# An attention kernel with Strassen's products: another order of the seven products, and q/k factors run in VectorE's pause before the softmax

## The chip, the cores and the metric

The kernel runs on one core of one Trainium2 chip. The metric is the device time of one execution in microseconds (us); of several executions the median is given. Smaller is better. All data is float32.

## The reference, cut to what matters

```python
# x: (4, 1024, 1024), cond: (4, 1024), 16 heads of 64
scale, shift = split(cond[:, None] @ W_emb + b_emb)
xn  = rms_norm(x, g_norm) * (1 + scale) + shift
q, k, v = heads(xn @ W_qkv)                  # 1024 -> 3 x 1024
q, k = rms_norm(q, g_q), rms_norm(k, g_k)    # over the 64 of a head
o = softmax(q @ k.T * 64**-0.5) @ v
x = x + o + o @ W_out
return x + causal_conv(x, w=cond, b)         # four taps along the tokens
```

The change touches the product `xn @ W_qkv` and the norm of q and k. The weights g_q and g_k are folded into k; what is left of the norm is one factor per token and head, 1 / sqrt(mean of squares), here called the factor of q and k.

## The kernel before, in words

**Work and stages.** For each of four batches the normalized, modulated x is written transposed to DRAM as four blocks (A11, A12, A21, A22) and sums of them (S1 to S4), in the form of Strassen and Winograd. A *double* is four heads: two *pairs* of heads of 128 columns each. Its q, k and v (2 x 384 columns, 1024 tokens) come from seven block products P1 to P7, each of four pieces of 128 tokens: 28 pieces a double (`PRODUCTS`, L480 to L485), 16 doubles. A piece is a group of matmuls into one of three PSUM accumulators (`ps_m`) and an eviction by ScalarE or VectorE (`Double.piece`, L537). The combined weight blocks T1 to T4 of a double's columns are made once, in batch 0 (`Weights.combine`, L468: four subtractions and four stores), and read back from DRAM (`load_w`, L499).

**The pair.** A pair's q and k come in two halves g of 512 tokens. `ENDS` (L570) says which product completes which half. `done` (L394) then books four steps: squares on ScalarE, sums on VectorE, a root on ScalarE, and `scale` on VectorE (L417: a reciprocal and one multiplication of the half by its factors). `transposes` (L422) turn q and k by TensorE, some pieces after the last product of the half (`LEADS`, L837); it calls `need`, which runs what is still booked for this half at once.

**The unit.** A unit (`Unit`, L573) is 512 queries of a pair; a double has four. It makes eight score tiles [128 keys, 2 heads, 512 queries]: TensorE, copy by ScalarE (L592), running maximum by VectorE (L601). Then POOL makes one all-reduce of the maximum over the partitions (L606), ScalarE copies it to PSUM into one of the two buffers of the score tiles (L615), and for each tile VectorE subtracts it (L620, the shift), ScalarE takes the exponential (L624) and POOL adds it to the sum (L626). In the next unit the values products (L646) and the product of ones with the sum (`tot`, L666) follow.

**The order.** Instructions of TensorE, VectorE, ScalarE and POOL run in the order in which the program issues them. The program keeps a clock of its own (`clock`, L92): each step that feeds TensorE moves it by an estimate (2.65 for a piece, 0.9 for a score tile), `defer` books a step for a due time, `tick` runs what is due. `defer_quiet` (L115) moves a due time out of the stretch in which shifts and exponentials run. `softmax` (L628) books the all-reduce at 2.6 after the last scores and the first shift at 7.6. While a unit of double n runs, seven pieces of double n+1 are placed between its steps (`between`, L940): unit i of the double gets pieces 7i to 7i+6, nearly all of them after the last scores. From batch 1 on a unit also carries one block of the output product and the convolution of the batch before; in the last batch these blocks are spread unevenly.

In the order of before, of the two pairs of a double the second (`px`) gets its first half from P2 (piece 7) and its second from P4 (piece 27); the first (`py`) gets its halves from P3 (piece 19) and P7 (piece 23).

```python
PRODUCTS: P1 P1 P2 P2 P1 P1 P2 P2, then 4 x P6, P5, P3, P7, P4
WEIGHTS = {"P1": -8, "P2": -4, "P6": 0, "P5": 6, "P3": 8, "P7": 12, "P4": 16}
ENDS = {"P2": (1, 0), "P3": (0, 0), "P7": (0, 1), "P4": (1, 1)}
LEADS = ((4, 4), (7, 7))          # [pair][half], in pieces
QUIET_QK = ((0, 0), (1, 1))
```

Of the kernel before, what the change touches and what calls it, by code (L numbers as in the profile page):

```python
# [10 lines left out]
F32 = mybir.dt.float32  # L11
AF = mybir.ActivationFunctionType
ALU = mybir.AluOpType
# [8 lines left out]
def kernel(  # L22
# [87 lines left out]
        clock[0] += us  # L110
        flush(lambda e: e[0] <= clock[0])

    loud = [0.0, 0.0]

    def defer_quiet(delay, key, step):  # L115

# [66 lines left out]
    class Norm:  # L183


        def __init__(self, b, tiles):
            self.b, self.tiles = b, tiles
            n = len(tiles)
            self.name = f"{b}_{tiles[0]}"
            self.ss = small.tile([P, NT * 2], F32, tag="ss", name=f"ss_{self.name}")  # L190
            self.ss = self.ss[:, : n * 2].rearrange("p (i g) -> p i g", i=n)
            self.rn = small.tile([P, NT], F32, tag="rn", name=f"rn_{self.name}")[:, :n]

# [109 lines left out]

    mod_sb = []
    x0 = {}
    homes = [("qTy0", 1), ("kTy0", 1), ("qTy1", 1), ("kTy1", 1), ("vy0", 1), ("vy1", 1), ("vx1", 2), ("vx1", 2)]

    def first_tokens(h):

# [62 lines left out]
    class Pair:  # L372
# [2 lines left out]
            self.qk = {}  # L375

        def begin(self):
            self.qT, self.kT, self.v = {}, {}, {}

        def open(self, g):  # L380

            b, c = self.b, self.c
            if g not in self.qk:
                self.qk[g] = apool.tile([P, HT, 2 * P], F32, tag="qk", name=f"qk_{b}_{c}_{g}", bufs=3)
                tag = f"v{'yx'[c % 2]}{g}"
                self.v[g] = apool.tile([P, HT, P], F32, tag=tag, name=f"v_{b}_{c}_{g}", bufs=1 + c % 2)

        def parts(self, t):

# [4 lines left out]
        def done(self, g):  # L394
            steps = ((0.6, self.squares), (2.2, self.sums), (4.2, self.root), (6.2, self.scale))
            for delay, step in steps:
                later = defer_quiet if step == self.scale and QUIET_QK[self.c % 2][g] else defer
                later(delay, ("qk", self.b, self.c, g), lambda step=step: step(g))


        def squares(self, g):
# [5 lines left out]
                self.sq.append(sq)  # L407

        def sums(self, g):
            self.ms = small.tile([P, 4 * HT], F32, tag="ms", name=f"ms_{self.b}_{self.c}_{g}")  # L410
            for i in range(2):
                nc.vector.tensor_reduce(self.ms[:, 2 * HT * i : 2 * HT * (i + 1)], self.sq[i], AX.X, ALU.add)

        def root(self, g):
            nc.scalar.activation(self.ms, self.ms, AF.Sqrt, bias=eps, scale=1.0 / D)

        def scale(self, g):  # L417
            qk = self.qk[g].rearrange("p t (h d) -> p (t h) d", d=D)
            nc.vector.reciprocal(self.ms, self.ms)
            nc.vector.tensor_mul(qk, qk, self.ms.unsqueeze(2).to_broadcast([P, 4 * HT, D]))  # L420

        def transposes(self, g, s):  # L422

            b, c = self.b, self.c
            need("qk", b, c, g)
            tp = ps_m.tile([P, HN], F32, tag="m", name=f"qkt_{b}_{c}_{g}_{s}")
            for i in range(HT):
                nc.tensor.transpose(  # L428
                    tp[:, i * P : (i + 1) * P], self.qk[g][:, i, s * P : (s + 1) * P], ident
                )  # L430
            tag = ("qT", "kT")[s]
            bufs = 2 if c % 2 and g == 0 else 1
            dst = apool.tile([P, HN], F32, tag=f"{tag}{'yx'[c % 2]}{g}", name=f"{tag}_{b}_{c}_{g}", bufs=bufs)
            if s:
                nc.scalar.activation(dst, tp, AF.Identity, scale=gqk)
            else:
                nc.scalar.copy(dst, tp)
            (self.qT, self.kT)[s][g] = dst
# [10 lines left out]
    class Weights:  # L449
# [6 lines left out]
        def load(self):  # L456
            d, k = self.d, self.k
            self.b = {}
            for kh in range(2):
                for y in range(2):  # L460
                    t = apool.tile([P, HN], F32, tag="ob", name=f"b_{self.name}_{kh}_{y}", bufs=8)
                    self.b[kh, y] = t[:, :W3]
                    for s, src in enumerate(w_block(kh, 2 * d + 1 - y, k)):
                        nc.sync.dma_start(t[:, s * P : (s + 1) * P], src)
            if d:
                defer_quiet(5.0, ("B", d), self.combine)

        def combine(self):  # L468
            b11, b12, b21, b22 = (self.b[kh, y] for kh in range(2) for y in range(2))
# [10 lines left out]
    PRODUCTS = []  # L480
    for ts in ((0, 1), (2, 3)):
        PRODUCTS += [("P1", A11, t) for t in ts] + [("P2", A12, t) for t in ts]
    for name, a in (("P6", S2), ("P5", S1), ("P3", S4), ("P7", S3), ("P4", A22)):
        PRODUCTS += [(name, a, t) for t in range(HT)]
    NPR = len(PRODUCTS)  # L485

    WEIGHTS = {"P1": -8, "P2": -4, "P6": 0, "P5": 6, "P3": 8, "P7": 12, "P4": 16}
    TIME = 2.65

    class Double:  # L490
        def __init__(self, n):
# [5 lines left out]
            self.w, self.a, self.u2, self.u4 = {}, {}, {}, {}  # L497

        def load_w(self, name):  # L499
            b, d = self.b, self.d  # L500
            w = wpool.tile([P, KH, W3], F32, tag="w", name=f"w_{b}_{d}_{name}", bufs=3)
            self.w[name] = w
            block = {"P1": (0, 2 * d + 1), "P2": (1, 2 * d + 1), "P3": (1, 2 * d)}.get(name)
# [33 lines left out]
        def piece(self, i):  # L537

            name, place, t = PRODUCTS[i]
            py, px = self.pairs  # L540
            pm = ps_m.tile([P, 512], F32, tag="m", name=f"pqkv_{self.n}_{name}_{t}")[:, :W3]
            w, a = self.w[name], self.a[place, t // 2]
            for k in range(KH):
                nc.tensor.matmul(  # L544
                    pm,
                    a[:, k, t % 2 * P : (t % 2 + 1) * P],
                    w[:, k, :],
                    start=(k == 0),
                    stop=(k == KH - 1),
                )  # L550
            tick(TIME)
            if name == "P1":
                self.u2[t] = apool.tile([P, W3], F32, tag="u2", name=f"u2_{self.n}_{t}", bufs=HT)
                nc.scalar.copy(self.u2[t], pm)
            elif name == "P6":
                nc.vector.tensor_add(self.u2[t], self.u2[t], pm)
            elif name == "P5":
                self.u4[t] = apool.tile([P, W3], F32, tag="u4", name=f"u4_{self.n}_{t}", bufs=HT)
                nc.vector.tensor_add(self.u4[t], self.u2[t], pm)
            else:  # L560
                pr, g, u = {"P2": (px, 0, self.u2), "P3": (py, 0, self.u4), "P7": (py, 1, self.u4), "P4": (px, 1, self.u2)}[name]
                for dst, at in pr.parts(g * HT + t):
# [377 lines left out]
    def between(p):  # L940
# [6 lines left out]
        pl = last_plan if b == B - 1 else plan  # L947
        ks = range(sum(pl[:i]), sum(pl[: i + 1])) if b else ()
        slots[0].append((0.45, store))
# [149 lines left out]
```

## Time and profile before

| | us |
|---|---|
| three executions: median (lowest, highest) | 2998.19 (2994.96, 3001.06) |
| the profiled execution: its time | 2998.24 |
| its span, first to last instruction | 2996.4 |
| TensorE busy in it (PE) | 2844.6 |
| VectorE busy (DVE) | 2227.7 |
| ScalarE busy (ACT) | 1701.0 |
| GpSimd busy (POOL) | 1407.5 |

The mean clock that TensorE was granted was 0.982 of its full one. How to read the lines that follow: a group is line, engine, operation, output<-inputs, shape and count, then busy us and mean ns of one, then the idle time of the engine just before them and what ended it. In a timeline a line begins with its start and its length in us. `A <- B: total, times, longest` in a list of waits means that engine and line A stood idle until B was done. "issue" is time in which an engine waited for nothing that the profile shows.

The units of batch 0 begin at 167.5 us; those of batch 1 at 803.2, of batch 3 at 2203.1; the last double begins at 2691.8.

### The profile page before, as it was taken

Reading aid. Unit: us, or ns where it says so; the run is one execution under the profiler, and the core shown is the slowest. Engines: PE = TensorE matmul, PEld = TensorE weight load, DVE = VectorE, ACT = ScalarE, POOL = GpSimd, SP = SyncE. Lnnn points to the kernel's source line nnn. Section 1 sums busy time; section 2 is a strip of 40 time slices with the busy share of each in tenths; the row PEclk is TensorE's granted clock in tenths of the full one; section 3 lists DMA queues with packets and bytes.
Section 4 is the critical chain, followed back from the end, with each engine's and each line's share of the span. In section 5 each row is a group of like instructions: output and inputs, shape, how many; then the busy total and the mean of one; then the engine's idle time right before and its main releaser. Section 6 shows DMA issues by size and latency. Waiting matters only on the chain.

```text
span 2996.4 us, 32118 instructions
## 1 busy us (share of the span) xinstructions
PE 2844.6 (95%) x10601; PEld 1343.9 (45%) x10601; DVE 2227.7 (74%) x2563; ACT 1701.0 (57%) x2237; POOL 1407.5 (47%) x574
## 2 busy tenths in 40 slices
PE   7789898999999999999999999999999999999899
PEld 3444444444444444444444444544444444443344
DVE  3468787877867777887777777887877768787863
ACT  3145666665655657665565656765565656565432
POOL 2035553455554454455455544535555455554420
PEclk9999999999999999999999999999999999999999
DMA  7855454543333344643433444643443333323333
GB/s 274 283 167 161 145 179 142 180 138 99 115 116 117 123 145 159 193 151 124 125 115 116 131 138 136 200 147 103 130 146 105 99 92 127 109 78 110 106 95 113
DMA packets 401661, 414.51 MB, mean 138 GB/s; under 512 B 40480, under 2 KB 331608, under 8 KB 401496
## 3 DMA queue, kind: packets, MB, share of 16 engines
q1 hardware_dynamic: 401496, 412.46, 43.6%
q8 instruction: 85, 1.39, 0.2%
q14 instruction: 80, 0.66, 0.1%
HBM read 336.88 MB, written 75.48 MB: 138 GB/s over the span
## 4 chain that ended last, share of the span: by engine, by line
PE 69%; DVE 15%; ACT 5%; DMA 4%; POOL 3%; issue 3%; SPq 1%; DVEq 0%; POOLq 0%; ACTq 0%
PE pqkv_P L544 29%; PE po L776 12%; PE s L584 12%; PE pav L646 11%; DVE sp L620 3%; DVE mx L601 3%; DVE y L808 3%; POOL sum L626 2%; ACT sp L592 2%; PE qkt L428 1%; DVE r L299 1%; DMA a<-scrA 1%; DVE b L476 1%; PE tot L666 1%; POOL mb L606 1%
## 5 line engine op out<-in xcount | busy, mean ns | idle before, releaser
L544 PE MATMUL pqkv_P<-w_P,a 128*128 128x384 f32 x3584 | 1225.2, 495 | 30.9 <-ACT r L230 9.0
L626 POOL TENSOR_TENSOR sum<-sum,sp 128x1024 f32<-128x1024 f32 x384 | 993.3, 2587 | 41.7 <-ACT sp L624 14.9
L544 PEld LDWEIGHTS pqkv_P<-w_P,a 128*128 128x128 f32 x3584 | 674.5, 193 | 517.9 <-issue 71.8
L592 ACT COPY sp<-s 128x1024 f32<-128x1024 f32 x512 | 511.4, 1015 | 468.1 <-PE s L584 376.6
L620 DVE TENSOR_TENSOR sp<-sp,mbp 128x1024 f32<-128x1024 f32 x512 | 604.1, 1212 | 70.8 <-ACT mbp L615 70.5
L601 DVE TENSOR_TENSOR mx<-mx,sp 128x1024 f32<-128x1024 f32 x384 | 519.6, 1353 | 172.1 <-ACT sp L592 146.5
L606 POOL PARTITION_ALL_REDUCE mb<-mx x64 | 207.7, 3245 | 834.8 <-DVE mx L601 690.1
L624 ACT ACTIVATE sp<-sp 128x1024 f32<-128x1024 f32 x512 | 525.4, 1054 | 124.0 <-DVE sp L620 119.3
L584 PE MATMUL s<-qT,kT 64*128 64x512 f32 x2048 | 523.7, 628 | 44.1 <-ACT sp L592 28.1
L646 PE MATMUL pav<-sp,v 128*64 128x512 f32 x2048 | 472.1, 603 | 0.0
L776 PE MATMUL po<-ob,wo 128*128 128x512 f32 x992 | 438.8, 595 | 2.4 <-DMA ob<-scrO 1.6
L626 POOL TENSOR_TENSOR sum<-sp,sp 128x1024 f32<-128x1024 f32 x64 | 151.3, 2364 | 535.2 <-ACT sp L624 364.0
L808 DVE SCALAR_TENSOR_TENSOR y<-x,cols,y 128x512 f32<-128x512 f32 x192 | 334.8, 1744 | 76.8 <-ACT y L796 72.3
L584 PEld LDWEIGHTS s<-qT,kT 64*128 64x128 f32 x2048 | 174.0, 188 | 316.3 <-issue 186.1
L646 PEld LDWEIGHTS pav<-sp,v 128*64 128x64 f32 x2048 | 136.8, 138 | 322.2 <-issue 301.6
L776 PEld LDWEIGHTS po<-ob,wo 128*128 128x128 f32 x992 | 184.1, 191 | 211.2 <-issue 205.0
L601 DVE TENSOR_TENSOR mx<-sp,sp 128x1024 f32<-128x1024 f32 x64 | 120.7, 1886 | 81.0 <-ACT sp L592 81.0
L563 DVE TENSOR_TENSOR qk<-u,pqkv_P 128x256 f32<-128x256 f32 x256 | 105.7, 413 | 94.2 <-PE pqkv_P L544 87.9
L794 ACT COPY x<-po 128x512 f32<-128x512 f32 x64 | 37.5, 585 | 238.1 <-PE po L776 221.7
L615 ACT COPY mbp<-mb 128x1024 f32<-128x1024 f32 x64 | 65.2, 1019 | 81.3 <-POOL mb L606 80.9
L420 DVE TENSOR_TENSOR qk<-qk,ms 128x1024 f32<-128x1024 f32 x64 | 106.5, 1664 | 2.2
L428 PE MATMUL qkt<-ident,qk 128*128 128x128 f32 x512 | 81.8, 283 | 27.2 <-DVE qk L420 27.1
(82 smaller groups left out, 1636.6 us busy)
## 6 DMA issues: line engine op xcount, KB each, us to landing
a<-scrA SPq DMA_DIRECT2D x220, 512.0 KB
w_P<-scrB SPq DMA_DIRECT2D x64, 768.0 KB
w_P<-in_L_cond_W_qkv_dram SPq DMA_DIRECT2D x144, 256.0 KB
wo<-in_L_cond_W_out_dram SPq DMA_DIRECT2D x128, 256.0 KB
scrA<-r SPq DMA_DIRECT2D x29, 896.0 KB
xc<-in_x_dram SPq DMA_DIRECT2D x64, 256.0 KB
out_dram<-ot SPq DMA_DIRECT2D x64, 256.0 KB
rec<-scrR SPq DMA_DIRECT2D x124, 128.0 KB
```

The source lines that it names most:

```text
L428: nc.tensor.transpose(tp[:, i * P : (i + 1) * P], self.qk[g][:, i, s * P : (s + 1) * P], ident)
L544: nc.tensor.matmul(pm, a[:, k, t % 2 * P : (t % 2 + 1) * P], w[:, k, :], start=(k == 0), stop=(k == KH - 1),)
L584: nc.tensor.matmul(ps[:, h, :], pr.kT[kt // HT][h * D : (h + 1) * D, kt % HT * P : (kt % HT + 1) * P], pr.qT[self.half][h * D : (h + 1) * ...
L592: nc.scalar.copy(sp, ps)
L601: nc.vector.tensor_max(self.mx, self.mx if kt > 1 else self.sp[0], self.sp[kt])
L606: nc.gpsimd.partition_all_reduce(self.mb.rearrange("p h q -> p (h q)"), self.mx.rearrange("p h q -> p (h q)"), P, bass_isa.ReduceOp.max,)
L620: nc.vector.tensor_sub(self.sp[kt], self.sp[kt], self.mb)
L624: nc.scalar.activation(sp, sp, AF.Exp)
L626: nc.gpsimd.tensor_tensor(self.sum, self.sum if kt > 1 else self.sp[0], sp, ALU.add)
L646: nc.tensor.matmul(self.pav[h * D : (h + 1) * D, :], self.pr.v[kt // HT][:, kt % HT, h * D : (h + 1) * D], self.sp[kt][:, h, :], start=(kt ...
L776: nc.tensor.matmul(self.pm, self.w[kh][:, k % KH, :], oTs[b, k, half], start=False, stop=(k == NJ - 1),)
L808: nc.vector.scalar_tensor_tensor(self.y, self.x1[:, k : k + HN], cols[:, r : r + 1], self.y, ALU.mult, ALU.add)
```

## The change

Four things, all in the order of issue; no operation is added or taken away.

1. The products come in the order P1, P2, P6, P7, P4, P5, P3. The roles of the two pairs are exchanged (`px, py = self.pairs`, and the weight columns with them): the first pair of a double gets its halves from P2 (piece 7) and P4 (piece 19), the second its second half from P5 (piece 23) and its first from P3 (piece 27). P7 now makes the partial sum u3, and P5 the additions that P7 made. `LEADS` grow to 11, 7, 10 and 9 pieces.
2. `defer_gap` books a step without a due time; `fill_gap`, booked 0.1 after the all-reduce, runs those that have waited long enough, up to 6.5 us of estimated length. `scale` goes there (1.5 each; the first double excepted), and `combine` for the weight columns of doubles 2 and 3 (2.5 each). `QUIET_QK` goes. A step that `need` asks for still runs at once.
3. `LATER` books all four steps of the second pair's first half 4 us later.
4. Buffers: one copy of q and k for each pair and half (before, two for one of them), two of v for each (before one or two), three of the factors `ms` and one of the norm's sums `ss` (before two each).

```diff
+    NEVER = 1e9
+    idle, loud = [], [0.0, 0.0]
+    def defer_gap(delay, key, us, step):
+        entry = (NEVER, next(serial), key, step)
+        pending.append(entry)
+        idle.append((clock[0] + delay, us, entry))
+    def fill_gap(us):
+        for e in list(idle):
+            if e[2] not in pending:
+                idle.remove(e)
+            elif e[0] <= clock[0] and e[1] <= us:
+                us -= e[1]
+                idle.remove(e)
+                pending.remove(e[2])
+                e[2][3]()
...
-            self.ss = small.tile([P, NT * 2], F32, tag="ss", name=f"ss_{self.name}")
+            self.ss = small.tile([P, NT * 2], F32, tag="ss", name=f"ss_{self.name}", bufs=1)
...
-                tag = f"v{'yx'[c % 2]}{g}"
-                self.v[g] = apool.tile([P, HT, P], F32, tag=tag, name=f"v_{b}_{c}_{g}", bufs=1 + c % 2)
+                self.v[g] = apool.tile([P, HT, P], F32, tag=f"v{c % 2}{g}", name=f"v_{b}_{c}_{g}", bufs=2)
...
             for delay, step in steps:
-                later = defer_quiet if step == self.scale and QUIET_QK[self.c % 2][g] else defer
-                later(delay, ("qk", self.b, self.c, g), lambda step=step: step(g))
+                delay += LATER[self.c % 2][g]
+                key = ("qk", self.b, self.c, g)
+                if step == self.scale and (self.b or self.c > 1):
+                    defer_gap(delay, key, 1.5, lambda: self.scale(g))
+                else:
+                    defer(delay, key, lambda step=step: step(g))
...
-            bufs = 2 if c % 2 and g == 0 else 1
-            dst = apool.tile([P, HN], F32, tag=f"{tag}{'yx'[c % 2]}{g}", name=f"{tag}_{b}_{c}_{g}", bufs=bufs)
+            dst = apool.tile([P, HN], F32, tag=f"{tag}{c % 2}{g}", name=f"{tag}_{b}_{c}_{g}", bufs=1)
...
             if d:
-                defer_quiet(5.0, ("B", d), self.combine)
+                if d > 1:
+                    defer_gap(5.0, ("B", d), 2.5, self.combine)
+                else:
+                    defer_quiet(5.0, ("B", d), self.combine)
...
-    for name, a in (("P6", S2), ("P5", S1), ("P3", S4), ("P7", S3), ("P4", A22)):
+    for name, a in (("P6", S2), ("P7", S3), ("P4", A22), ("P5", S1), ("P3", S4)):
...
-    WEIGHTS = {"P1": -8, "P2": -4, "P6": 0, "P5": 6, "P3": 8, "P7": 12, "P4": 16}
+    WEIGHTS = {"P1": -8, "P2": -4, "P6": 0, "P7": 6, "P4": 8, "P5": 12, "P3": 16}
...
-            py, px = self.pairs
+            px, py = self.pairs
...
-            elif name == "P5":
-                self.u4[t] = apool.tile([P, W3], F32, tag="u4", name=f"u4_{self.n}_{t}", bufs=HT)
-                nc.vector.tensor_add(self.u4[t], self.u2[t], pm)
+            elif name == "P7":
+                self.u3[t] = apool.tile([P, W3], F32, tag="u3", name=f"u3_{self.n}_{t}", bufs=HT)
+                nc.vector.tensor_add(self.u3[t], self.u2[t], pm)
             else:
-                pr, g, u = {"P2": (px, 0, self.u2), "P3": (py, 0, self.u4), "P7": (py, 1, self.u4), "P4": (px, 1, self.u2)}[name]
+                pr, g, u = {"P2": (px, 0, self.u2), "P4": (px, 1, self.u3), "P5": (py, 1, self.u3), "P3": (py, 0, self.u2)}[name]
                 for dst, at in pr.parts(g * HT + t):
                     nc.vector.tensor_add(dst, u[t][:, at], pm[:, at])
-                if name == "P7":
+                if name == "P5":
                     nc.vector.tensor_add(self.u2[t], self.u2[t], pm)
...
-    ENDS = {"P2": (1, 0), "P3": (0, 0), "P7": (0, 1), "P4": (1, 1)}
+    ENDS = {"P2": (0, 0), "P4": (0, 1), "P5": (1, 1), "P3": (1, 0)}
...
             defer(TO_MAX, key, self.maximum)
+            defer(TO_MAX + 0.1, key, lambda: fill_gap(GAP))
...
-    LEADS = ((4, 4), (7, 7))
+    LEADS = ((11, 7), (10, 9))
...
-    QUIET_QK = ((0, 0), (1, 1))
+    LATER = ((0, 0), (4, 0))
+    GAP = 6.5
```

More of the change, by code (lines that the diff above doesn't have):

```diff
@@ L111, in tick @@
         flush(lambda e: e[0] <= clock[0])
-    loud = [0.0, 0.0]
+    NEVER = 1e9
[13 more added lines that the diff above has]
+                e[2][3]()
     def defer_quiet(delay, key, step):
@@ L305 @@
     x0 = {}
-    homes = [("qTy0", 1), ("kTy0", 1), ("qTy1", 1), ("kTy1", 1), ("vy0", 1), ("vy1", 1), ("vx1", 2), ("vx1", 2)]
+    homes = [("qT00", 1), ("kT00", 1), ("qT01", 1), ("kT01", 1), ("v10", 2), ("v10", 2), ("v11", 2), ("v11", 2)]
     def first_tokens(h):
@@ L377, in begin @@
         def begin(self):
-            self.qT, self.kT, self.v = {}, {}, {}
+            self.qT, self.kT, self.v, self.ms = {}, {}, {}, {}
         def open(self, g):
@@ L409, in sums @@
         def sums(self, g):
-            self.ms = small.tile([P, 4 * HT], F32, tag="ms", name=f"ms_{self.b}_{self.c}_{g}")
+            self.ms[g] = small.tile([P, 4 * HT], F32, tag="ms", name=f"ms_{self.b}_{self.c}_{g}", bufs=3)
             for i in range(2):
-                nc.vector.tensor_reduce(self.ms[:, 2 * HT * i : 2 * HT * (i + 1)], self.sq[i], AX.X, ALU.add)
+                nc.vector.tensor_reduce(self.ms[g][:, 2 * HT * i : 2 * HT * (i + 1)], self.sq[i], AX.X, ALU.add)
         def root(self, g):
-            nc.scalar.activation(self.ms, self.ms, AF.Sqrt, bias=eps, scale=1.0 / D)
+            nc.scalar.activation(self.ms[g], self.ms[g], AF.Sqrt, bias=eps, scale=1.0 / D)
         def scale(self, g):
             qk = self.qk[g].rearrange("p t (h d) -> p (t h) d", d=D)
-            nc.vector.reciprocal(self.ms, self.ms)
-            nc.vector.tensor_mul(qk, qk, self.ms.unsqueeze(2).to_broadcast([P, 4 * HT, D]))
+            nc.vector.reciprocal(self.ms[g], self.ms[g])
+            nc.vector.tensor_mul(qk, qk, self.ms[g].unsqueeze(2).to_broadcast([P, 4 * HT, D]))
         def transposes(self, g, s):
@@ L462, in load @@
                     self.b[kh, y] = t[:, :W3]
-                    for s, src in enumerate(w_block(kh, 2 * d + 1 - y, k)):
+                    for s, src in enumerate(w_block(kh, 2 * d + y, k)):
                         nc.sync.dma_start(t[:, s * P : (s + 1) * P], src)
             if d:
-                defer_quiet(5.0, ("B", d), self.combine)
+                if d > 1:
+                    defer_gap(5.0, ("B", d), 2.5, self.combine)
+                else:
+                    defer_quiet(5.0, ("B", d), self.combine)
         def combine(self):
@@ L496, in __init__ @@
                 pr.begin()
-            self.w, self.a, self.u2, self.u4 = {}, {}, {}, {}
+            self.w, self.a, self.u2, self.u3 = {}, {}, {}, {}
         def load_w(self, name):
@@ L502, in load_w @@
             self.w[name] = w
-            block = {"P1": (0, 2 * d + 1), "P2": (1, 2 * d + 1), "P3": (1, 2 * d)}.get(name)
+            block = {"P1": (0, 2 * d), "P2": (1, 2 * d), "P3": (1, 2 * d + 1)}.get(name)
             if block:
@@ L947, in between @@
         pl = last_plan if b == B - 1 else plan
+        slots[0].append((0.45, store))
         ks = range(sum(pl[:i]), sum(pl[: i + 1])) if b else ()
-        slots[0].append((0.45, store))
         if b and i == 0:
```

## The prediction

> **What bounds the kernel now.** I began with the page's engine row and then cut the span into five stages by the starts of units (one unit: softmax of 512 queries of a pair of heads): the start, the units of batch 0, of batches 1 and 2, of batch 3 up to its last four, and the tail. In the answer for these stages the columns are length, then PE, PEld, DVE, ACT and POOL busy, the granted clock, the DMA share and GB/s.
>
> ```profile
> PE 2844.6 (95%) x10601; PEld 1343.9 (45%) x10601; DVE 2227.7 (74%) x2563; ACT 1701.0 (57%) x2237; POOL 1407.5 (47%) x574
> ```
>
> ```profile
> 0.00:167.50 167.50, 130.46 (x423) 65.47 (x423) 66.36 (x155) 35.85 (x79) 16.95 (x22) 0.93 0.84 279
> 167.50:803.20 635.70, 577.67 (x2202) 271.28 (x2201) 506.19 (x576) 400.98 (x513) 334.55 (x126) 0.97 0.45 145
> 803.20:2203.10 1399.90, 1383.23 (x5247) 660.59 (x5246) 1088.48 (x1219) 860.58 (x1141) 696.64 (x288) 1.00 0.44 138
> 2203.10:2691.80 488.70, 475.45 (x1801) 223.39 (x1800) 373.65 (x412) 285.42 (x340) 263.40 (x104) 0.99 0.33 104
> 2691.80:2996.40 304.60, 277.79 (x937) 123.22 (x936) 192.97 (x203) 118.21 (x166) 95.93 (x37) 0.96 0.35 104
> ```
>
> TensorE is the bound, and its work doesn't change. Only its idle time can be won: length minus PE is 37.0, 58.0, 16.7, 13.3 and 26.8 us, 151.8 in all. So the question is which of these holes the edits can close. The waits of TensorE alone name them (us in total, times, longest):
>
> ```profile
> PE s L584 <- ACT sp L592: 28.1, 38, 2.2
> PE qkt L428 <- DVE qk L420: 27.1, 8, 8.0
> PE s L584 <- DVE sp L620: 15.8, 9, 4.1
> PE tot L666 <- POOL sum L626: 13.7, 7, 6.6
> ```
>
> **Edit 1, order and leads.** Products, operands, evictions and loads keep their number: P7 loses its two extra additions and P5 gains them, in the same piece numbers (20 to 23). The first pair of heads is now complete after piece 19 instead of 23; its last transposes come at pieces 26 and 27, seven after its last product, instead of 27 and 28, four after. The other pair's come at 32, 33, 37, 38 instead of (14, 15) and 34, 35. The wait for the scale of q and k is what the lead governs:
>
> ```profile
> 482.12 1.09 PE L428 MATMUL qkt<-ident,qk 128*128 128x128 f32 x4 [8.00 <-DVE qk L420]
> ```
>
> This is the transpose at piece 27, three pieces after P7. By stage the waits of qkt for L420 are 19.0 us in batch 0 (four), 7.2 in batch 3 (three) and 0.9 at the start. In the new order the scale runs in the pause of a unit before its transposes, so I count all of 26.2 (19.0 + 7.2) as gone.
>
> **Edit 2, LATER = 4 for the second pair's first half.** The half that ends with piece 27 starts its squares at the next unit's first scores. In the timeline of ScalarE and of TensorE at such a unit:
>
> ```profile
> 981.75 1.28 ACT L415 ACT_TABLE_LOAD   x1
> ...
> 984.37 0.31 ACT L415 ACTIVATE ms<-ms,eps 128x16 f32<-128x16 f32 x1 [1.33 <-DVE ms L412]
> ...
> 985.62 2.04 PE L584 MATMUL s<-qT,kT 64*128 64x512 f32 x8 [2.12 <-ACT sp L592]
> ```
>
> ScalarE stands in its queue at the root, waiting for VectorE's sums (L412), which stand behind a maximum; behind the root stand the copies that free the score buffers, and TensorE waits 2.12. In first units of doubles these holes are 1.92, 1.16, 0.65 and 1.33 in batch 0; 2.12, 2.06, 1.62, 2.12, 2.06 and 1.61 in the middle; 0.89 and 2.19 later: 19.7 us together. Later by 4 us of the kernel's own clock, the root falls after the sixth score tile, ahead of the second half of the values products, when no score copy is due at once. I count all but 1.7 as gone: 18. The bounds are 0 (the same collision, later) and 19.7.
>
> **Edit 3, scale and combine in VectorE's pause.** From the last maximum to the first shift VectorE waits for the all-reduce (3.25) and its copy (1.02): about 4.6 us. The new list runs scale there, and for the columns of doubles 2 and 3 the four subtractions of combine. Elsewhere these pay for POOL's additions:
>
> ```profile
> L420 DVE TENSOR_TENSOR qk<-qk,ms 128x1024 f32<-128x1024 f32 x64 | 106.5, 1664 | 2.2
> ...
> L476 DVE TENSOR_TENSOR b<-b,b 128x384 f32<-128x384 f32 x48 | 45.8, 953 | 24.7 <-DMA b<-in_L_cond_W_qkv_dram 23.5
> ...
> 288.20 8.55 DVE L476 TENSOR_TENSOR b<-b,b 128x384 f32<-128x384 f32 x4
> ```
>
> Medians by the lines' own views are 1226 and 558 ns, so 64 x 0.44 + 48 x 0.395 = 28 + 19 = 47 us of VectorE time is blocking. It is not on the path as such (VectorE is 74% busy), but the 8.55 us for four subtractions stand ahead of the maxima of that unit. In its place stands what the pause costs. Here the Trainium skill speaks against the edit: "SBUF — State Buffer", section "Who interferes with whom", says that a VectorE instruction with two SBUF inputs and a GpSimd instruction that reads SBUF exclude each other for a whole instruction. The all-reduce reads SBUF, and scale and combine have two SBUF inputs. The rows inside such pauses:
>
> ```profile
> 224.98 3.25 POOL L606 PARTITION_ALL_REDUCE mb<-mx  x1 [7.46 <-DVE mx L601]
> ...
> 227.48 2.33 DVE L476 TENSOR_TENSOR b<-b,b 128x384 f32<-128x384 f32 x4
> ...
> 1309.35 3.17 DVE L299 TENSOR_TENSOR r<-r 128x256 f32<-128x256 f32 x4
> ...
> 1309.67 3.25 POOL L606 PARTITION_ALL_REDUCE mb<-mx  x1 [16.22 <-PE pqkv_P L544]
> ```
>
> Four subtractions took 2.33, no more than four times the median, with one wholly beside the all-reduce, which kept its 3.25; four of L299 took 3.17 where a free group at 1266.45 took 1.55. So it is free or costs 1.6, not the all-reduce's whole length. I take the free price: scale 0.25 + 1.22 = 1.47, combine 2.33.
>
> Load of a pause, after what is in it already (0.2 to 2.8 us; it has some 4.6): in batches 1 to 3 the units of a double receive two, none, one and one scale, that is 3.0, 0, 1.5, 1.5: they fit. In batch 0's second and third doubles combines join: third unit two combines and a scale, 6.1 with 0.7 present, over by 2.2; fourth unit 3.8 with 2.3, over by 1.5; the following first unit 5.3 with 0.2, over by 0.9. That is 4.6 a double, 9.2 for two. I charge it fully, because the last shift releases the PSUM buffer of the broadcast maximum that the next unit's second scores need (L584 waits for L620, above), and batch 0 has no room there. POOL's sum hides it: it starts 8.4 us after the all-reduce in the mean (535.2 / 64), and at 1000 us its second exponential ended 3.5 us before POOL began. If fills were blocked as the rule has it, the over-full pauses would grow by about 2.5 each (6 units) and the all-reduce start about 1 us late in the nine units of batch 0 where POOL's sum sets the row-sum product: 15 + 9 = 24 us more, and a time of 2982.
>
> For the gain: TensorE's waits for evictions in batch 0 (L565 6.0, L556 2.3, L559 2.3 = 10.6) come from VectorE's backlog in just those units; I take half, 5.3, between 0 and 10.6. A fill ahead of the evictions in its queue delays them by at most 6 us, with three accumulators of 2.65 us a piece: taken as zero, up to 1 us a double (16 us) if the cover is gone. Each combine also issues four stores on SP, which wait for the pause with the loads queued behind them; the loads have cover (operands are asked for four pieces ahead, the first product that reads the new columns comes eight pieces, 21 us, after its load): zero, or 2 us for each of eight combines.
>
> **Edit 4, buffers.** q and k of the second pair's first half go from two copies to one, v from one or two to two each. Their writers now come after the last reader: the transposes at 32, 33, 37, 38 lie in the units after the pair's last scores. The norm's sums lose a copy used once a batch. SP's loads keep their places; in the first double T3 and T4 are asked for earlier (6 and 8 instead of 12 and 16), but their stores were issued by 73.9 us and the loads start from 80.9. All taken as zero; plus or minus 2 us at the start.
>
> **The sum.** Gained: 26.2 + 18 + 5.3 = 49.5. Given back: 9.2. Net 40, against 2998.24 for the profiled execution (span 2996.4), which is the median of the runs, 2998.19. Forecast 2958. By stage: about -20 in batch 0, -11 in the middle, -8 in batch 3 and -2 in the tail.
>
> **Rivals.**
> *Batch 0 gives its part back* (2977). There POOL's sum ends within 0.5 us of the product that reads it in nine of sixteen units: the units from 326.5 to 436.6 last 36 to 37 us, by TensorE and by the chain maximum, all-reduce, sum alike. If that chain doesn't shorten, only 21 us from the other stages remain. For it: tot's 13.7 us lie wholly in batch 0. Against: the long waits (8.00, 3.66) lie in units where POOL was done 5.8 to 9.5 us early.
> *The late last shift* (3014, slower). Fills, and the evictions behind them, make the last shift d later, and the PSUM buffer of the maximum holds up the next scores. It has no slack in batch 0 (16 units) and 0.5 to 4 us in the fourth unit of each later double (12 units); 28 units x 2 us = 56 against 40 gained. It decides from d = 1.45. For it: L584 waits for L620 already. Against: the fourth unit's pause has 5.3 us with 2.7 busy, and 1.5 fits.
> *The waits only change their name* (2998): the steps are due late, and transposes force them out at the last moment, so qkt waits for the scale as before. Against: every pause lies four or more pieces ahead of its transposes.
>
> **Chances.** Main case 0.70, at 2958, its own range 2942 to 2972; batch 0 gives back 0.16; name changed 0.06; slower 0.08. Against a measurable 0.2% (6 us): faster 0.86, same 0.06, slower 0.08. The range 2938 to 2984 takes in the first two, the eviction cover and the blocked price.
>
> **What would show it.** Right: no qkt wait for L420; L420 near 1230 ns and L476 near 560 in the mean, apart from early ones; holes of 2 us at first units gone; TensorE idle some 38 us in batch 0, 6 in the middle. Wrong: L620 starting over 6 us after the last maximum in most units, larger waits of L584 for L620 or of L666 for L626, or an all-reduce much longer than 3.25.

## The result, and the profile after

The changed kernel took 2969.36 us (median of four executions, 2966.98 to 2978.04) beside 2999.62 for the kernel before on the same chip (2994.96 to 3002.53): a ratio of 0.9906, 95% interval 0.9881 to 0.9931. It is faster by 30 us where 40 was forecast. The profiled execution took 2966.98, with a span of 2965.2 and a mean granted clock of 0.989 (before 0.982). From L299 on (now L317) lines stand 18 to 24 further down: L428 is now L449 (qkt), L420 L441 (the scale's multiplication), L476 L499 (combine), L584 L607 (scores), L592 L615 (their copies), L606 L629 (the all-reduce), L615 L638 (its copy), L620 L643 (the shift), L626 L649 (POOL's sum), L646 L670 (values), L666 L690 (`tot`).

The engine row of the page, after:

```profile
PE 2830.4 (95%) x10601; PEld 1335.5 (45%) x10601; DVE 2234.6 (75%) x2563; ACT 1694.0 (57%) x2233; POOL 1401.2 (47%) x574
```

The stages after, cut at the same units, with the same columns as before:

```profile
0.00:170.00 170.00, 132.28 (x419) 66.45 (x419) 68.15 (x155) 35.05 (x78) 16.89 (x22) 0.92 0.83 276
170.00:776.70 606.70, 566.89 (x2201) 265.91 (x2200) 501.17 (x573) 394.41 (x509) 330.99 (x124) 0.99 0.48 151
776.70:2181.20 1404.50, 1382.99 (x5245) 659.73 (x5244) 1090.57 (x1221) 860.40 (x1142) 705.76 (x293) 1.00 0.44 138
2181.20:2663.60 482.40, 472.48 (x1801) 221.81 (x1800) 378.97 (x413) 285.43 (x340) 258.76 (x104) 1.00 0.34 105
2663.60:2965.20 301.60, 275.73 (x941) 121.60 (x940) 195.71 (x204) 118.68 (x165) 88.81 (x34) 0.97 0.36 105
```

| | start | batch 0 | batches 1, 2 | batch 3 | tail |
|---|---|---|---|---|---|
| length before | 167.5 | 635.7 | 1399.9 | 488.7 | 304.6 |
| length after | 170.0 | 606.7 | 1404.5 | 482.4 | 301.6 |
| measured | +2.5 | -29.0 | **+4.6** | -6.3 | -3.0 |
| forecast | 0 | -20 | **-11** | -8 | -2 |
| TensorE idle, before | 37.0 | 58.0 | 16.7 | 13.3 | 26.8 |
| TensorE idle, after | 37.7 | 39.8 | 21.5 | 9.9 | 25.9 |

Two things are to be seen. The forecast failed in one stage, the middle, which got longer. And TensorE was busy for 14.2 us less on the same 10601 instructions (2844.6 to 2830.4), most of it in batch 0 (577.67 to 566.89), where the granted clock rose from 0.97 to 0.99. The idle time fell by 17.0; the two together are the 31.2 by which the span shrank.

The longest waits of TensorE over the whole span, after:

```profile
PE s L607 <- ACT sp L615: 23.1, 59, 2.5
PE s L607 <- DVE sp L643: 16.2, 10, 4.5
...
PE tot L690 <- POOL sum L649: 7.7, 3, 4.4
```

No wait of the transposes of q and k for the scale is left, as forecast. The scores' wait for ScalarE's copies fell only from 28.1 to 23.1, and it now comes 59 times instead of 38. The wait for the late shift (L643) stayed where it was, 15.8 to 16.2.

The group of the all-reduce from the page, then those of scale and combine from the groups by line, after:

```profile
L629 POOL PARTITION_ALL_REDUCE mb<-mx x64 | 223.9, 3499 | 850.4 <-DVE mx L624 499.7
```

```profile
L441 DVE TENSOR_TENSOR qk<-qk,ms 128x1024 f32<-128x1024 f32 x64 | 123.2, 1924 | 2.2
...
L499 DVE TENSOR_TENSOR b<-b,b 128x384 f32<-128x384 f32 x48 | 35.8, 745 | 25.0 <-DMA b<-in_L_cond_W_qkv_dram 23.7
```

The multiplication was to fall from 1664 to some 1230 ns in the mean; it rose to 1924. The all-reduce grew from 3245 to 3499. What happens in such a pause is seen in the timeline of all engines at the first unit of a double, after:

```profile
1145.29 1.22 DVE L441 TENSOR_TENSOR qk<-qk,ms 128x1024 f32<-128x1024 f32 x1
1145.33 4.29 POOL L629 PARTITION_ALL_REDUCE mb<-mx  x1 [19.52 <-DVE ms L440]
...
1146.71 2.64 DVE L441 TENSOR_TENSOR qk<-qk,ms 128x1024 f32<-128x1024 f32 x1
```

The first multiplication was running when the all-reduce began: it kept its 1.22, and the all-reduce took 4.29 instead of 3.25. The second began inside the all-reduce and took 2.64 instead of 1.22. So the two do hold each other up, whichever comes second. But the second multiplication ended (1149.35) before the all-reduce did (1149.62): it was not kept out for all of it.

### The profile page after: what moved, and what is told of

It is laid out like the page before. It is cut to its first block, busy times and chain, and to the rows that moved or that the text cites. A ratio compares the mean times of both kernels' runs of the same rounds, so it can differ in the third digit from the quotient of the medians.

```text
span 2965.2 us, 32084 instructions
## 1 busy us (share of the span) xinstructions
PE 2830.4 (95%) x10601; PEld 1335.5 (45%) x10601; DVE 2234.6 (75%) x2563; ACT 1694.0 (57%) x2233; POOL 1401.2 (47%) x574
## 5 line engine op out<-in xcount | busy, mean ns | idle before, releaser
L649 POOL TENSOR_TENSOR sum<-sum,sp 128x1024 f32<-128x1024 f32 x384 | 974.1, 2537 | 60.2 <-ACT sp L647 34.0
L615 ACT COPY sp<-s 128x1024 f32<-128x1024 f32 x512 | 510.7, 1015 | 460.9 <-PE s L607 363.9
L624 DVE TENSOR_TENSOR mx<-mx,sp 128x1024 f32<-128x1024 f32 x384 | 526.6, 1371 | 217.7 <-ACT sp L615 193.1
L643 DVE TENSOR_TENSOR sp<-sp,mbp 128x1024 f32<-128x1024 f32 x512 | 604.8, 1212 | 33.7 <-ACT mbp L638 33.5
L629 POOL PARTITION_ALL_REDUCE mb<-mx x64 | 223.9, 3499 | 850.4 <-DVE mx L624 499.7
L607 PE MATMUL s<-qT,kT 64*128 64x512 f32 x2048 | 519.5, 624 | 39.4 <-ACT sp L615 23.1
L670 PE MATMUL pav<-sp,v 128*64 128x512 f32 x2048 | 472.4, 604 | 0.0
L832 DVE SCALAR_TENSOR_TENSOR y<-x,cols,y 128x512 f32<-128x512 f32 x192 | 320.6, 1670 | 111.3 <-ACT y L820 106.8
L649 POOL TENSOR_TENSOR sum<-sp,sp 128x1024 f32<-128x1024 f32 x64 | 151.3, 2364 | 478.4 <-ACT sp L647 288.3
L607 PEld LDWEIGHTS s<-qT,kT 64*128 64x128 f32 x2048 | 171.2, 186 | 331.4 <-issue 168.3
L670 PEld LDWEIGHTS pav<-sp,v 128*64 128x64 f32 x2048 | 136.9, 138 | 321.4 <-issue 309.5
L624 DVE TENSOR_TENSOR mx<-sp,sp 128x1024 f32<-128x1024 f32 x64 | 131.5, 2055 | 84.5 <-ACT sp L615 83.5
L638 ACT COPY mbp<-mb 128x1024 f32<-128x1024 f32 x64 | 65.1, 1017 | 122.4 <-POOL mb L629 122.4
L441 DVE TENSOR_TENSOR qk<-qk,ms 128x1024 f32<-128x1024 f32 x64 | 123.2, 1924 | 2.2
L427 ACT ACTIVATE sq<-qk 128x512 f32<-128x512 f32 x128 | 76.1, 626 | 62.8 <-DVE qk L586 62.7
```

The costliest lines, as they stand in the source:

```text
L441: nc.vector.tensor_mul(qk, qk, self.ms[g].unsqueeze(2).to_broadcast([P, 4 * HT, D]))
L607: nc.tensor.matmul(ps[:, h, :], pr.kT[kt // HT][h * D : (h + 1) * D, kt % HT * P : (kt % HT + 1) * P], pr.qT[self.half][h * D : (h + 1) * ...
L615: nc.scalar.copy(sp, ps)
L624: nc.vector.tensor_max(self.mx, self.mx if kt > 1 else self.sp[0], self.sp[kt])
L629: nc.gpsimd.partition_all_reduce(self.mb.rearrange("p h q -> p (h q)"), self.mx.rearrange("p h q -> p (h q)"), P, bass_isa.ReduceOp.max,)
L643: nc.vector.tensor_sub(self.sp[kt], self.sp[kt], self.mb)
```

## The experiments

Each run's ratio is to the kernel before on the same chip (medians of 2997.4 to 3001.9). Stages are those of one profiled execution of each run: batch 0, middle (batches 1 and 2), batch 3. The theories that the expectations letter are these. For the middle: the transposes of q and k left their place between two score tiles, where they had covered ScalarE's copies (theory A from the first series on); the rival is the pause, with VectorE and GpSimd in each other's way. For the gain: the whole of it comes from edit 2.

| run | median (lowest, highest) | ratio [95%] | batch 0 | middle | batch 3 |
|---|---|---|---|---|---|
| the change | 2969.36 (2966.98, 2978.04) | 0.9906 [0.9881, 0.9931] | 606.7 | 1404.5 | 482.4 |
| e1_later0 | 3006.23 (2998.94, 3012.51) | 1.0023 [1.0013, 1.0032] | 625.5 | 1420.1 | 485.3 |
| e2_combine_due | 2968.63 (2964.88, 2970.07) | 0.9900 [0.9884, 0.9916] | 611.0 | 1405.9 | 482.3 |
| e3_scale_due | 2975.60 (2969.22, 2976.81) | 0.9921 [0.9906, 0.9936] | 619.0 | 1401.5 | 484.9 |
| e4_piece_early | 2965.37 (2961.81, 2969.47) | 0.9892 [0.9875, 0.9909] | 614.4 | 1401.9 | 480.4 |
| e6_no_multiply | 2957.05 (2954.97, 2959.16) | 0.9854 [0.9838, 0.9871] | 604.6 | 1400.9 | 481.9 |
| e7_before_later | 2968.52 (2965.39, 2975.30) | 0.9895 [0.9878, 0.9912] | 631.9 | 1380.4 | 487.6 |
| e8_leads_fill | 2957.85 (2955.43, 2961.83) | 0.9858 [0.9841, 0.9876] | 614.1 | 1390.9 | 480.6 |
| e9_no_pause | 2982.07 (2980.27, 2987.51) | 0.9937 [0.9922, 0.9951] | 623.4 | 1406.9 | 484.9 |
| e10_chunks_aside | 2964.59 (2960.88, 2969.74) | 0.9891 [0.9873, 0.9910] | 618.9 | 1391.9 | 480.7 |
| e11_old_combine_pause | 2966.84 (2954.43, 2974.13) | 0.9895 [0.9872, 0.9918] | 617.4 | 1380.2 | 484.7 |
| e12_fill_first | 2964.15 (2960.61, 2970.29) | 0.9894 [0.9875, 0.9913] | 618.7 | 1393.6 | 482.0 |
| e13_chunks_due | 2955.94 (2949.68, 2957.80) | 0.9870 [0.9852, 0.9889] | 615.1 | 1386.0 | 480.9 |

**First series: one edit undone at a time.**

Edit 2 undone:

```diff
-    LATER = ((0, 0), (4, 0))
+    LATER = ((0, 0), (0, 0))
```

> The changed kernel with LATER set to zero: the second pair's first half books its root 4 us earlier again. Theory A (the 11.6 us of root waits in the middle stage did go, and something else took them back): the waits of about 2 us at the first unit of a double return, middle stage +11, total +13 to +18 us, some 2984. Theory B (the booking doesn't matter in the new order, the pause is what counts): within 4 us of 2969.

Measured: 37 us slower than the change, and 7 slower than before: without edit 2 the rest gains nothing. Both theories had this edit too small. The scores' wait for the copies doubled to 48.3 us, 20.7 of it in the middle.

Combine by its due time again, out of the pause:

```diff
-                    defer_gap(5.0, ("B", d), 2.5, self.combine)
+                    defer_quiet(5.0, ("B", d), self.combine)
```

> The changed kernel with combine booked by due time as before, scale still in the pause. Theory A (in batch 0 most of the 29 us come from the subtractions leaving the way of the maxima): batch 0 longer by 10 to 15 us, nothing elsewhere, total near 2981. Theory B (overfull pauses cost more than they give): batch 0 shorter by 4 to 8, total near 2963.

Measured: no difference (2968.63). Neither theory had that; taking combine alone out of the pause costs nothing that shows.

Scale by its due time again:

```diff
-                    defer_gap(delay, key, 1.5, lambda: self.scale(g))
+                    (defer_quiet if self.c % 2 else defer)(delay, key, lambda: self.scale(g))
```

> The changed kernel with scale booked by due time as before (out of the shifts for the second pair only), combine still in the pause. Theory A: the middle stage stays within 3 us of 1404.5, because what took its gain is not in the pause; total 2966 to 2976. Theory B (the lock between the multiplication and the all-reduce, 1.92 us a multiplication and 3.50 an all-reduce, ate the middle's gain): the middle stage is shorter by about 10, total near 2959.

Measured: 6 us slower, with intervals that overlap, so this is not clear of noise; by the stages it would lie in batch 0 (+12.3, though the change's own 606.7 is the second lowest of all these executions). The middle moved by 3, where theory B asked for 10: the scale in the pause is not what the middle lost.

One piece of the products more between the score tiles (`BEHIND` is the estimated length of the pieces kept for after the last scores):

```diff
-    BEHIND = 25
+    BEHIND = 24.6
```

> The changed kernel with BEHIND 24.6 instead of 25, so that in units of batch 1 and later a first piece stands between the score tiles again. Theory A (the emptied score phase costs 0.31 us of wait and 0.37 us in all in each unit, since four score tiles in a row run at the pace of ScalarE's copies): 44 units x 0.37, middle shorter by 8 to 9, batch 3 by 4, total near 2957. Theory B: no change, 2969.

Measured: 4 us faster, inside the intervals, where theory A asked for 12. The waits for the copies fell to 10.9, in the middle from 7.4 to none. Five of the middle's eight doubles do show it: 170.4 us each, where the change takes 171.3 to 172.2. In this execution the rest of the middle hid it: it has four spells of 3.41 us at half clock (the change three) and one wait of 3.5 in the output product (the change 1.9).

**Second series: what the middle lost, and where the gain is.**

The multiplication by the factors cut to one of 64 columns:

```diff
-            nc.vector.tensor_mul(qk, qk, self.ms[g].unsqueeze(2).to_broadcast([P, 4 * HT, D]))
+            nc.vector.tensor_mul(qk[:, :, :1], qk[:, :, :1], self.ms[g].unsqueeze(2))
```

> The changed kernel with the multiplication by the factors cut to one of 64 columns (q and k stay unscaled in the others): the length of the scale step and its lock on the all-reduce are gone, all else stays. Theory A (the middle stage lost its gain in the emptied score phase, not in the pause): middle stage within 4 us of 1404.5, total 2960 to 2970, the little there is coming from batch 0. Theory B (the pause and its lock cost it): middle shorter by 8 or more, total below 2957.

This kernel leaves most of q and k unscaled. Measured: 12 us faster than the change, but the middle only by 3.6. Even with nearly none of this work in the pause the middle, 1400.9, is no shorter than it was before any of the edits (1399.9). The pause can account for no more than a few us of the middle.

Edit 2 alone, in the kernel before (there the second pair's half that ends last is the other one):

```diff
+                delay += LATER[self.c % 2][g]
...
+    LATER = ((0, 0), (0, 4))
```

> The kernel before with one thing of the change: the four steps of the half that ends with piece 27 (there P4's) booked 4 us later. Without that booking the change measured 3006, so: theory C (the booking is worth its 37 us only in the new order, where nothing stands between the score tiles to hide the wait): the 19.7 us of root waits go, near 2980. Theory D (the booking alone is the gain, and order and pause bring next to nothing): as fast as the change, 2963 to 2973.

Measured: 2968.52, as fast as the whole change. Its waits and its middle stage:

```profile
PE qkt L429 <- DVE qk L421: 25.4, 8, 6.3
PE tot L667 <- POOL sum L627: 18.8, 8, 4.7
```

```profile
801.80:2182.20 1380.40, 1376.68 (x5245) 659.23 (x5244) 1098.51 (x1219) 861.53 (x1142) 698.77 (x288) 1.00 0.45 140
```

The middle has 3.7 us of idle time left (before 16.7, the change 21.5), while the waits for the scale are all still there, in batches 0 and 3, and the product with the sum waits longer (18.8; before 13.7).

The leads set so that the transposes of q and k fall into the score phase again:

```diff
-    LEADS = ((11, 7), (10, 9))
+    LEADS = ((13, 8), (7, 18))
```

> The changed kernel with LEADS ((13, 8), (7, 18)): in each unit one of the two transposes again comes first of its pieces and falls between the score tiles. Theory A: the four score tiles in a row (4.21 us for 16 matmuls) become two and two with the transposes between, 0.3 to 0.4 us a unit less in 44 units, and the eight waits of 0.37 for the k copy go: middle near 1393, batch 3 some 4 less, total near 2954. Theory B (pause): no change, 2965 to 2971.

Measured: 2957.85, the middle shorter by 13.6. TensorE's timeline in a score phase, first of the change:

```profile
1658.19 1.99 PE L607 MATMUL s<-qT,kT 64*128 64x512 f32 x8
1660.43 2.04 PE L607 MATMUL s<-qT,kT 64*128 64x512 f32 x8 [0.25 <-ACT sp L615]
1662.41 3.65 PE L670 MATMUL pav<-sp,v 128*64 128x512 f32 x16
```

then of this run:

```profile
959.88 1.99 PE L607 MATMUL s<-qT,kT 64*128 64x512 f32 x8
961.80 0.66 PE L449 MATMUL qkt<-ident,qk 128*128 128x128 f32 x4
962.38 1.99 PE L607 MATMUL s<-qT,kT 64*128 64x512 f32 x8
964.30 1.94 PE L670 MATMUL pav<-sp,v 128*64 128x512 f32 x8
```

In the change four score tiles in a row take 4.22 (1658.19 to 1662.41), since the third needs the buffer that ScalarE still copies. With four transposes between, they take 4.42 (959.88 to 964.30), of which 0.58 is the transposes' own work (961.80 to 962.38): 0.38 us less for the scores in each such unit. In the change 24 of the middle's 32 units have four in a row, here none: 24 x 0.38 = 9.1 of the 13.6. The rest is about what three half-clock spells cost (see below), which the change has in its middle and this run has not. Its middle:

```profile
782.40:2173.30 1390.90, 1378.17 (x5247) 659.50 (x5246) 1094.59 (x1220) 862.88 (x1144) 707.65 (x292) 1.00 0.45 139
```

Scale and combine both out of the pause (the diffs of the second and third run together):

> The changed kernel with neither scale nor combine in the pause (both booked by due time, scale out of the shifts for the second pair). If the two parts add up, e3's 6 us and e2's nothing: near 2975. If the pause's worth is hidden in their overlap (either alone is absorbed): 2980 or more. If overfull pauses cost more than they give: below 2969.

Measured: 2982.07, 12.7 slower than the change, more than the two apart (0 and 6). That either alone is still covered by the other was one of the expectations; how is not shown. It is 13.5 slower than edit 2 alone: without the pause, the new order loses.

**Third and fourth series: what is left in the middle.** Of its eight doubles two carry the loading of the next batch's tokens (chunks). Those take 187.4 and 185.6 us in the change, 180.3 each in e7 and 185.1 in e8. From e8, the transposes of the chunks moved to other pieces:

```diff
+    CHUNKS = (1, 4, 8, 10, 12, 16, 19, 22)
...
-                elif i % 3 == 1 and i < 24:
-                    s = i // 3
+                elif i in CHUNKS:
+                    s = CHUNKS.index(i)
```

> e8 with the transposes of the next batch's chunks moved off the pieces where the transposes of q and k now fall (pieces 1, 4, 8, 10, 12, 16, 19, 22 for 1, 4, 7, 10, 13, 16, 19, 22). In the kernel before with the late booking alone such a double took 180.3 us, in e8 185.2, in the change 187.4, while other doubles are alike in e7 and e8 (169.8 and 169.6). Theory A (three transposes in one piece's place fill the three accumulators): four such doubles, the two of the middle shorter by 3 to 5 each, middle near 1383, total near 2950. Rival (the chunks' VectorE sums or loads are what is late there): within 4 us of e8.

Measured: a miss. The units of those doubles stayed as they were (46.8, 48.1, 45.9, 44.3; e8 46.8, 48.2, 45.9, 44.3), and the total rather rose (by 7; the intervals just touch).

Edit 2 in the old order with combine in the pause (e7, and `defer_gap`, `fill_gap` and the change's line for combine):

```diff
+            defer(TO_MAX + 0.1, key, lambda: fill_gap(6.5))
```

> The kernel before with the late booking (e7) and with combine in the pause, order and leads of before. Theory P (the subtractions ahead of the maxima, 8.55 us for four at 288.2, are what batch 0 suffers from in the old order): batch 0 shorter by 8 to 14, total near 2958. Theory Q (as in the new order, where combine in or out of the pause made no difference): within 4 us of 2968.5.

Measured: inconclusive. The profiled execution has batch 0 shorter by 14.5, but it was the fastest of six that lie between 2954 and 2974; the median is e7's.

From e10, a piece more between the scores in batch 0:

```diff
-    BEHIND_FIRST = 20.0
+    BEHIND_FIRST = 19.4
```

> e10 with BEHIND_FIRST 19.4 for 20, so that in batch 0 too a transpose falls between the score tiles. If the pace of ScalarE's copies counts there as in the middle: 0.3 us a unit, 5 us less than e10. If batch 0 is held by the chain maximum, all-reduce, shift, sum: no change from e10.

Measured: no change from e10 (batch 0 618.7 and 618.9), though 15 of its 16 units now have such work between the scores, and five before. Batch 0 doesn't hang on the pace of the copies.

From e8, the scale by its due time in the chunk doubles alone:

```diff
+                if step == self.scale and self.c in (5, 6) and self.b < B - 1:
+                    (defer_quiet if self.c % 2 else defer)(delay, key, lambda: self.scale(g))
```

> e8 with the factors of the pairs whose pause lies among the next batch's chunk transposes booked by due time; all others stay in the pause. With scale in the pause the four units at the start of such a stretch took 48.6, 45.8, 48.8 and 44.2 us in the change, without it (e9) 45.9, 45.9, 47.1 and 44.1: 4.4 less, because the two multiplications and the lengthened all-reduce hold back evictions for which the chunk transposes wait (1.88 at 1150.7). Theory A (that is what the pause costs): the two such stretches of the middle shorter by 2 to 4 each than e8's 185.2, middle near 1385, total near 2952 at e8's chances. Rival (with e8's leads the accumulators are held by something else, as e10's unchanged 185.1 says): middle within 2 us of 1390.8.

Measured: those doubles 182.5 instead of 185.1, the middle 4.9 shorter; the total, 2955.94, is not told apart from e8's. (The 4.4 that this expectation starts from holds a half-clock spell as well: the change's other chunk double is only 2.5 longer than e9's.)

## Why the prediction was right and wrong

**The total, and luck.** That 2969 came out near the forecast 2958 is in part luck: two errors of opposite sign. Edit 2, forecast at 18, gives all of the gain alone (e7 2968.52). Of the 22.3 that edits 1 and 3 were to add (26.2 + 5.3 - 9.2) nothing is left in the total; what they won in batches 0 and 3 went again in the middle.

**"TensorE's work doesn't change. Only its idle time can be won": wrong.** The work is the same, its duration isn't. TensorE's timeline of before holds the same hole that the prediction read, at another unit:

```profile
1681.08 0.66 PE L428 MATMUL qkt<-ident,qk 128*128 128x128 f32 x4
1683.86 3.54 PE L584 MATMUL s<-qT,kT 64*128 64x512 f32 x8 [2.12 <-ACT sp L592]
```

and the stretches around it (length, the five engines, then the granted clock):

```profile
1682.00:1686.00 4.00, 2.14 (x6) 1.12 (x8) 3.59 (x4) 2.61 (x4) 1.99 (x1) 0.70 0.02 4
1686.00:1690.00 4.00, 4.00 (x18) 1.02 (x18) 3.10 (x4) 2.02 (x2) 0.00 (x0) 0.87 0.00 0
```

Eight score matmuls that take 1.99 elsewhere took 3.54 here: the two stretches lack 0.30 x 4 + 0.13 x 4 = 1.7 us of work at full clock, on top of the 2.12; at half clock that is a spell of 3.4 us. Summed from the trace's records of the granted clock, half-clock time fell from 109.9 us to 66.8; at half clock that is up to 21.5 us of work, and busy TensorE time fell by 14.2. The clock's records give spells of 3.41, three in the middle of before. The Trainium skill ("TensorE: Matmul & The Clock Gate", section "HAM oscillation — how this bites in real kernels") gives the rule "no PE-idle gaps >~3.4µs". By that rule a hole of 2.12 costs 2.12. Here three of the four holes of 2.06 to 2.12 in the middle came with such a spell and cost some 3.8 (2.12 + 1.7, an estimate); those of 1.33, 1.61 and 1.62 did not. The measurement decides.

**Edit 2, "I count all but 1.7 as gone: 18": right in mechanism, but little more than half of what it brought.** Alone it brought 33 us (e7 against its own before, 3001.88 to 2968.52), in the new order 37 (e1 to the change). In the middle, where nothing else moves in e7, the stage lost 19.5: 13.0 of idle time and 6.5 of busy time. The holes were read right: the prediction lists 11.6 there, and the one of 1.33 that it puts under batch 0 ends at 812.61, in batch 1; that makes 12.9. What the sum lacked is the clock, which a list of holes can't show: three spells of 3.41 in the middle of before, worth 1.7 each, and none in e7's. Between the profiled executions e7's span is 27.2 shorter, with 3.8 more from batch 0 and 5.2 from the tail; that the medians differ by 33 lies within the scatter of single executions.

**Edit 1, "I count all of 26.2 as gone": right for the waits, wrong for the time.** The waits are gone, and batch 0 and batch 3 are 29.0 and 6.3 shorter than before; from e7, where edit 2 is in already, still 25.2 and 5.2 shorter, by edits 1, 3 and 4 together. What failed is a step that the prediction didn't take: of the transposes it moved it asked where they go and not what they had covered where they were. Set in the middle of a run of four score tiles they gave ScalarE the time to copy; four score tiles in a row run at the copies' pace. TensorE's waits in the middle: for the copies before and in e7, then the longest in the change:

```profile
PE s L584 <- ACT sp L592: 13.6, 10, 2.1
```

```profile
PE s L585 <- ACT sp L593: 0.2, 1, 0.2
```

```profile
PE s L607 <- ACT sp L615: 7.4, 24, 1.0
PE xtp L301 <- DVE v L586: 4.3, 4, 1.9
PE pqkv_P L567 <- ACT qT L457: 3.4, 2, 1.7
PE pqkv_P L567 <- ACT kT L455: 2.9, 8, 0.4
```

The six doubles of the middle without chunks take 1031.5 us together in the change, 1019.7 in e7, and 1020.7 with the transposes set back (e8): 11.8 lost against e7. Of this, 24 units x 0.38 = 9.1 lies in the score phase; a wait of 0.37 a double for the copy of k makes 2.2. The two chunk doubles (187.4 and 185.6, in e7 180.3 each) add 12.4. Together this is the middle's distance from e7 (1404.5 - 1380.4 = 24.1).

The emptied score phase explains the first part alone: no unit of a chunk double makes four score tiles in a row. There TensorE waits 7.2 us more than in e7: mostly chunk transposes (`xtp`) behind VectorE's evictions, and pieces behind ScalarE's copy of q. And it is busy for 5.3 us more on the same work: the three half-clock spells of the change's middle all lie in these two doubles, at holes of 1.88 and 1.71. So edits 1, 3 and 4 won some 30 us in batches 0 and 3 and lost 24 in the middle. In the medians nothing is left: 2969.36 beside e7's 2968.52.

**Edit 3, "I take the free price": wrong; the lock that I weighed against it is there, but not for an instruction's whole length.** The rows I argued from hid it: with the all-reduce at 224.98 to 228.23 and the subtractions from 227.48, only 0.75 us lay side by side. In the changed kernel 38 of the 64 multiplications begin inside the all-reduce and take 2.40 in the mean; two that begin in its last 0.2 us keep their 1.22; and when one begins just before it (15 times), that one takes 1.22 and the all-reduce 4.29. "Over by 2.2, 1.5, 0.9" in batch 0's full pauses became 3.9, 2.2 and 2.1 (first shift 8.5, 6.8 and 6.7 us after the last maximum, where the pause has 4.6). A combine inside one, after:

```profile
259.74 3.25 POOL L629 PARTITION_ALL_REDUCE mb<-mx  x1 [6.64 <-DVE mx L624]
259.88 2.16 DVE L499 TENSOR_TENSOR b<-b,b 128x384 f32<-128x384 f32 x1
```

One subtraction of 0.56 took 2.16. In the new order the edit still pays: without both, the kernel is 12.7 slower (e9). Outside batch 0 the price is small: a pause with one multiplication mostly keeps its 4.6 us, one with two mostly grows to 5.6. What multiplication and lock cost together is bounded by e6: 12 us.

**By stage.** Batch 0, "about -20": -29.0, with the clock's part (10.8 of busy time) that I had not counted. There edits don't add up: edit 2 alone brings 3.8, the rest alone 10.2 (e1), both 29.0, by single executions. That with one set of waits gone another takes part of the time is seen in e7 (the product's wait for the sum, 18.8 after 13.7); the rest is not shown. Middle, "-11": +4.6, above. Batch 3 and tail, "-8" and "-2": -6.3 and -3.0. **Edit 4, "zero":** no run isolates it, and nothing speaks against it: e8 has it and takes 169.7 for a double where e7, without it, takes 169.8 (five of the six without chunks); the start's +2.5 is in e7 too (169.9).

**The rivals.** Batch 0 did not give its part back, the late last shift did not come (L643: 16.2 us; in 53 of 64 units the first shift starts within 6 us of the last maximum), and the waits did not keep their place under another name. The loss that did come, in a stage where no wait for the scale stood, was none of them.

**Open.** What makes the chunk doubles wait in the new order: e13 takes back 2.6 of e8's 4.8 us each over e7 (185.1, 182.5, 180.3), the rest is unexplained; how batch 0's 25 us beyond e7 divide between order and pause (e9 gives 8.5 and 16.7, from single executions); and whether combine in the pause helps the old order (e11).

The best versions measured are e8 and e13, at 2957.85 and 2955.94: ratios of 0.9858 [0.9841, 0.9876] and 0.9870 [0.9852, 0.9889].

## What to carry to other kernels

When work is moved, price the place that it leaves as well as the place that it goes to: filler between two steps that share a buffer may be all that hides the copy between them. A hole on the busiest engine can cost more than the list of waits says, so compare the durations of the same instructions behind it. Before an overlap is taken as free, find out for how much of the two rows they lay side by side.

## What the runs showed of the hardware

- Short holes in TensorE's stream came with half clock. Of four holes of 2.06 to 2.12 us in the middle of the kernel before, three came with a spell of 3.41 us at half clock (score matmuls 3.54 instead of 1.99); of five of 1.71 to 1.88 in the middle of the changed kernel, three. In e8 two of 1.82 came with none, so the length of a hole alone doesn't decide. Half-clock time was 109.9 us in the kernel before, 66.8 in the changed one and 87.4 in e7.
- A two-input multiplication on VectorE and the all-reduce on GpSimd hold each other up, and the later one pays: 1.22 became 2.0 to 2.6, or 3.25 became 4.3. The multiplication is not kept out for the whole 3.25.
- A score tile takes TensorE 1.0 us and its copy takes ScalarE 1.01. With two buffers, four tiles in a row took 4.22; with 0.58 us of other work in their middle they took 3.84, that work taken off.
